# Two transformer layers on one core: where the gate of layer 0 is folded, when the weight additions are sent, and how the gate's rows are multiplied

## The chip, the core and the metric

The kernel runs on one core of a Trainium2 chip. The core has five engines that run their own queues in order and wait for each other through semaphores: TensorE (PE in the profile, its weight loads PEld), VectorE (DVE), ScalarE (ACT), GpSimd (POOL), and SyncE (SP), which here only issues transfers. The metric is device time of the whole program in microseconds (us). Before the change three runs took 984.28, 980.25 and 982.10 us, a median of 982.1.

## What is computed

The reference adds two layers to x (8 batches of 256 rows of 512, float32). Only layer 0 is touched. Its conditioning is an attention with rotary positions over a window of 256 keys in a paged cache, and its feed-forward part is a gated sum of eight weight matrices, which differ in 4096 places:

```python
q = rope(rms(x @ Wq.T)); k = rope(rms(x @ Wk.T)); v = x @ Wv.T
# k and v are written into the cache's blocks at pos = kv_len + t
p = softmax(where(allowed, q @ k_all.T * SCALE, -inf))
h = concat_heads(p @ v_all) @ Wo.T                       # output of the attention

logits = clip(h @ gate_w.T, -50, 50)                     # 8 experts
top_w, top_idx = top_k(logits, 2);  rw = softmax(top_w)
weighted = (softmax(expert_atom_weights) @ atoms) * sigmoid(importance)   # 8 x 4096
vals = einsum('tk,tks->ts', rw, weighted[top_idx])
out = h @ W.T + segment_sum((h[:, cols] * vals).T, rows).T   # rows, cols from mask_idx
x = x + out
```

Layer 1 (a linear layer with low-rank adapters, then a mixture of eight experts, two per row) follows and isn't touched.

## The kernel before

**Tiles.** There are 16 tiles of 128 rows (NT), two to a batch; the 512 columns are four chunks of 128 (KC). All products are float32, and the profile records such a product as two records of PE; a transpose through PE is one.

**Projection (from L1147).** For each tile, `keys_values` (L1153) multiplies x by the weights of keys and values, rotates the keys on VectorE and stores them to kv_new in HBM. Beside it the eight weight matrices are laid out in HBM: `spread_base` (L1186) copies the common matrix eight times side by side and stores it to delta_d (16 stores, issued by SP), and `sum_same` (L1276) and `find_places` (L1301) find the sums and the places of the 4096 entries, in 32 columns. `add_delta` (L1127) sends one column of 128 entries to delta_d, as an indirect transfer that adds, issued by POOL. Six of these (BESIDE) are sent in the projection's loop, at tiles 8 to 13. The weights woT (output projection) and gw (gate) are fetched at tile 8 by `later` (L1307).

At its end the projection makes the queries of batches 0 and 1: `query_rows` (L1092) multiplies and rotates, `queries_turned` (L1114) transposes on PE and copies out with ScalarE.

**Fold.** The gate sees only the attention's output, so its weights are multiplied with the output projection once: gwo = Wo.T @ gate_w.T, 512 x 8. Before the attention's loop (L1490 to L1509) the four blocks of woT are transposed (pw), copied out (won), and each serves as the stationary operand of four products with 8 columns (pgo):

```python
for k in range(KC):
    nc.tensor.matmul(pgo[k], won[:, k * P : (k + 1) * P], gw[:, d, :], start=(d == 0), stop=(d == KC - 1))
```

**Attention (loop over 8 batches, from L1526).** Batch b works on keys and values that were gathered by POOL into kv_rows[b] (`gather_old` from the cache, `gather_new` from kv_new, four indirect transfers each), two batches ahead. `prepared` transposes the next batch's keys (KT) and makes its masks, `queries` projects the batch after next, `attend` makes scores (ps), softmax on VectorE and ScalarE (s), transposes (pp, pT) and products with values (po), for one tile and eight heads at a time. Between a batch's two tiles five of the remaining additions (LATER) are issued by POOL; each of them waits until the one before has landed.

After a batch's two tiles, `gate_rows(i)` (L1476) makes the logits of one tile: four products with a 128 x 128 stationary piece of the attention's output oT and the 8 columns of gwo, summed in PSUM, then one VectorE operation clips them into lg0. `output_rows` (L630) multiplies the tile by woT and stores h. Then the queries of batch b + 2 are turned.

**What sets the order.** The source gives dependences; a planner with costs of its own orders each engine's instructions when the program is built, and each engine then runs its list strictly in that order. PSUM is cut into pools with a fixed number of buffers: in the projection psq (3), psd (3, and two single buffers pw0 and pw1), in the attention ps_s (2), ps_p (2) and ps_o (2, tag misc, shared by pg, ph, pk, pt, po). `in_a_row` (L107) keeps the products given to it next to each other, so that products on different halves or quarters of the array's columns can run side by side. `seen_through` (L116) is a helper that layer 1 uses for its own fold: it is printed below.

Of the kernel before, what the change touches and what calls it, by code (L numbers as in the profile page):

```python
# [19 lines left out]
P = 128  # L20
B, T, D = 8, 256, 512
# [3 lines left out]
KC = D // P  # L25
# [6 lines left out]
E = 8  # L32
# [3 lines left out]
NSC = NS // P  # L36
# [45 lines left out]
def two_layer_kernel(ctx: ExitStack, tc: tile.TileContext, io: dict, out: bass.AP):  # L82
    nc = tc.nc
# [514 lines left out]
    ost = ExitStack()  # L598
    op = ost.enter_context(tc.tile_pool(name="op", bufs=1, side="right"))
    woT = op.tile([P, KC, D], F32, name="woT")  # L600
    gwo = op.tile([P, KC, E], F32, name="gwo")
    oTs = {}

    def load_delta(half, pool, engines, bufs, tag="raw", paced=False):
# [41 lines left out]
    with ExitStack() as att:  # L646
        ap = att.enter_context(tc.tile_pool(name="ap", bufs=1))
# [7 lines left out]
        sums = place_ap.tile([P, NSC, E], F32, name="sums")  # L655
# [9 lines left out]
        minus_half = ap.tile([P, 1], F32, name="minus_half")  # L665
        nc.gpsimd.memset(minus_half, -0.5)

        gw = ap.tile([P, KC, E], F32, name="gw")
        epss = ap.tile([P, 2], F32, name="epss")
        nc.gpsimd.memset(epss[:, 0:1], EPS)  # L670
        nc.gpsimd.memset(epss[:, 1:2], EPS / (SCALE * SCALE))
# [442 lines left out]
        def queries_turned(qrs, psum, tag):  # L1114

            QT = qtp.tile([P, KC, T], F32, name="QT")
            for t, qr in enumerate(qrs):
                qflat = qr.rearrange("p h d -> p (h d)")
                pt = psum.tile([P, KC, P], F32, name="pt", tag=tag)
                for m in range(KC):  # L1120
                    nc.tensor.transpose(
                        pt[:, m, :], qflat[:, m * P : (m + 1) * P], ident
                    )
                nc.scalar.copy(QT[:, :, t * P : (t + 1) * P], pt)
            return QT

        def add_delta(k, values):  # L1127

            nc.gpsimd.indirect_dma_start(
                out=delta_d,  # L1130
                out_offset=bass.IndirectOffsetOnAxis(ap=put_i[:, k : k + 1], axis=0),
                in_=values,
                in_offset=None,
                bounds_check=D * D + P - 1,
                oob_is_err=True,
                compute_op=ALU.add,
            )
# [2 lines left out]

        roots = ap.tile([P, NT, H], F32, name="roots")

        BESIDE = 6
        LATER = 5


        with proj:  # L1147
# [159 lines left out]
            def later(tile, src, rs):  # L1307

                nc.scalar.copy(tile[:, 0, :1], rs[:, :1])
                nc.sync.dma_start(tile, src)  # L1310

            FIRST = 8
            summed = placed = 0
            for i in range(LEAD, NT):
                rs = keys_values(i)
                if i == LEAD:
                    with_gains(qcos, qsin, "q_scale")
                    rot.close()
# [12 lines left out]
                for k in range(summed, min(summed + 3, NSC)):  # L1331
                    sum_same(k)
                    summed = k + 1
                if summed - placed >= 8 or i == NT - 1:
                    find_places(range(placed, summed))
                    placed = summed
                if i >= FIRST and i - FIRST < BESIDE:
                    add_delta(i - FIRST, sums[:, i - FIRST, :])
            gather_new(0)

            qq = proj.enter_context(tc.tile_pool(name="qq", bufs=2, side="right"))
            QTs = {}
            for b in range(2):
                rows = [
                    query_rows(
                        i, blocks[NTB][:, :, i * P : (i + 1) * P], psq, "pkv", qq, early=True
                    )
                    for i in range(2 * b, 2 * b + 2)
                ]
                QTs[b] = queries_turned(rows, psd, "psd")  # L1350


        otp = ost.enter_context(tc.tile_pool(name="otp", bufs=1, side="right"))
# [119 lines left out]
                if m % 2:  # L1473
                    next(beside, None)

        def gate_rows(i):  # L1476
            pg = ps_o.tile([P, E], F32, name="pg", tag="misc")
            for k in range(KC):
                nc.tensor.matmul(
                    pg,  # L1480
                    oTs[i // 2][:, k, (i % 2) * P : (i % 2 + 1) * P],
                    gwo[:, k, :],
                    start=(k == 0),
                    stop=(k == KC - 1),
                )
            nc.vector.tensor_scalar(lg0[:, i, :], pg, 50.0, -50.0, ALU.min, ALU.max)

        AHEAD = 2

        with ExitStack() as fold:  # L1490
            fo = fold.enter_context(tc.tile_pool(name="fo", bufs=1))
            pgos = [ps_s.tile([P, 2, 512], F32, name="pgo", tag="ps") for j in range(KC // 2)]
            pgo = [pgos[k // 2][:, k % 2, :E] for k in range(KC)]
            for d in range(KC):
                pw = ps_o.tile([P, KC, P], F32, name="pw", tag="misc")
                for k in range(KC):
                    nc.tensor.transpose(pw[:, k, :], woT[:, k, d * P : (d + 1) * P], ident)
                won = fo.tile([P, D], F32, name="won")
                nc.scalar.copy(won, pw.rearrange("p c r -> p (c r)"))
                for k in range(KC):  # L1500
                    nc.tensor.matmul(
                        pgo[k],
                        won[:, k * P : (k + 1) * P],
                        gw[:, d, :],
                        start=(d == 0),
                        stop=(d == KC - 1),
                    )
            for k in range(KC):
                nc.scalar.copy(gwo[:, k, :], pgo[k])  # L1509

        gather_new(1)
        ready = prepared(0, kv_rows[0])
        zero = wop.tile([P, D], F32, name="zero")
# [12 lines left out]
        for b in range(B):  # L1526
            kvs = kv_rows[b]
            if b + AHEAD < B:
                if b + AHEAD > 2:
                    find_rows(b + AHEAD)  # L1530
                gather_old(b + AHEAD)
                gather_new(b + AHEAD)
            if b == B - 2:
                beside = load_delta(0, xq, (nc.scalar.copy,), 3, tag="xb", paced=True)
                next(beside)
            oTs[b] = otp.tile([P, KC, T], F32, name="oT", bufs=4)
            if b + 2 < B:
                qrs = queries(b + 2)
            if b < B - 2:
                start_sums(b)  # L1540
            if b == B - 3:
                start_sums(b + 1)
                start_sums(b + 2)
            if b == 1:
                for rest in (*sums_d, h_d, g_d):
                    nc.sync.dma_start(rest[N:, :], zero)
            attend(b, 0, kvs, QTs[b], *ready, beside)
            now = ready
            if b + 1 < B:
                ready = prepared(b + 1, kv_rows[b + 1])  # L1550
            ks = range(BESIDE + LATER * b, min(BESIDE + LATER * (b + 1), NSC))
            if ks:

                held = bp.tile([P, 1], F32, name="held")
                nc.vector.tensor_scalar(held, ready[1][:, 0, :1], 1.0, None, ALU.is_lt)
                entries = bp.tile([P, len(ks), E], F32, name="entries")
                nc.vector.tensor_scalar(
                    entries, sums[:, ks[0] : ks[-1] + 1, :], held, None, ALU.mult
                )
                for j, k in enumerate(ks):  # L1560
                    add_delta(k, entries[:, j, :])
# [560 lines left out]
```

## Time and profile before

One execution was profiled. It took 983.58 us, its span from the first to the last instruction is 981.7 us, and its mean clock granted to TensorE is 0.967 of full speed.

| Stretch of the span, us | Length | PE busy | DVE busy | ACT busy | POOL busy | clock |
|---|---|---|---|---|---|---|
| 0 to 80, start and projection | 80 | 69.68 | 57.50 | 45.49 | 32.85 | 0.96 |
| 80 to 88 | 8 | 6.19 | 4.00 | 5.21 | 0.00 | 0.57 |
| 88 to 111, projection's end | 23 | 20.90 | 20.85 | 14.20 | 8.80 | 1.00 |
| 111 to 129, fold and first query rows | 18 | 17.32 | 9.42 | 3.60 | 13.96 | 0.53 |
| 129 to 138 | 9 | 6.88 | 7.72 | 3.19 | 5.64 | 1.00 |
| 138 to 143 | 5 | 4.37 | 5.00 | 3.60 | 1.10 | 0.66 |
| 143 to 412, attention | 269 | 257.56 | 184.15 | 181.64 | 104.48 | 1.00 |
| 412 to 460, output rows and routing | 48 | 39.41 | 32.20 | 14.67 | 14.81 | 0.89 |

How to read the profile: a line of a list by time gives start and length in us, engine, line of the kernel, operation, output and inputs by the program's names with their shapes, and how many instructions are merged; in brackets stands the idle time of that engine before it and what released it. [...]the pace of a series is read from one start to the next. "DMA_INDIRECT" on POOL is a gather or a scatter[...].

### The profile page before, as it was taken

How to read it: one execution, taken by the hardware profiler on the slowest of the kernel's cores; microseconds unless marked ns; L12 is line 12 of the kernel's file. 1: busy time of each engine (PE TensorE's matmuls, PEld its weight loads, DVE VectorE, ACT ScalarE, POOL GpSimd, SP SyncE). 2: the span in 40 equal slices, each digit the busy share in tenths (PEclk: the TensorE clock that was granted, in tenths of full speed). 3: DMA queues.
4: the chain of work that ended last, by engine and by line, in shares of the span. 5: the costliest groups of instructions: out<-in, count | busy, mean ns of one | idle time of the engine just before them, and what ended most of it. 6: DMA issues, size and time to landing. Idle time of an engine off the chain costs nothing. (4 is left out here: it accounts for less than half of the span.)

```text
span 981.7 us, 14436 instructions
## 1 busy us (share of the span) xinstructions
PE 914.2 (93%) x4897; PEld 511.9 (52%) x4897; DVE 455.7 (46%) x1477; ACT 372.5 (38%) x958; POOL 357.2 (36%) x333
## 2 busy tenths in 40 slices
PE   6998889999999998897999997999599999999995
PEld 3554646556556565545433333545277777753332
DVE  5786789758548576583211111471012222323332
ACT  3675447547557489651111112410111111112321
POOL 2631655654554300123666652000223333333211
PEclk9898789999999999997999999999799999999998
DMA  6696494423441202256997766981433444343322
GB/s 192 216 320 236 123 306 143 115 59 82 118 126 28 93 19 70 84 195 226 344 308 139 126 111 144 357 315 43 171 74 67 70 73 73 65 75 62 49 28 37
DMA packets 74238, 134.63 MB, mean 137 GB/s; under 512 B 17309, under 2 KB 22941, under 8 KB 74032
## 3 DMA queue, kind: packets, MB, share of 16 engines
q0 software_dynamic: 25088, 43.68, 23.5%
q1 hardware_dynamic: 38496, 74.57, 21.9%
q10 hardware_dynamic: 10576, 15.39, 4.3%
q8 instruction: 42, 0.69, 0.3%
q14 instruction: 36, 0.29, 0.1%
HBM read 89.95 MB, written 52.56 MB: 145 GB/s over the span
## 5 line engine op out<-in xcount | busy, mean ns | idle before, releaser
L575 DVE COPY xsT<-pa 128x512 f32<-128x512 f32 x68 | 46.8, 688 | 155.6 <-PE pa L569 148.5
L533 POOL DMA_INDIRECT xs<-g_d,token_i_l x34 | 35.3, 1037 | 229.4 <-PE pa L569 129.4
L2014 DVE TENSOR_TENSOR y<-py,b 64x512 f32<-64x512 f32 (+1 forms) x46 | 31.7, 690 | 185.8 <-PE py L547 122.2
L1998 ACT ACTIVATE hs<-pu,b 128x64 f32<-128x64 f32 (+1 forms) x184 | 46.2, 348 | 185.8 <-PE pu L1972 144.4
L556 PE MATMUL py<-delta,xsT 128*64 128x512 f32 (+1 forms) x416 | 94.8, 598 | 0.0
L1439 ACT ACTIVATE s<-s,mx,roots 128x384 f32<-128x384 f32 x128 | 89.7, 705 | 12.2 <-DVE mx L1435 11.3
L1972 PE MATMUL pu<-xsT,w 128*128 128x128 f32 x704 | 82.9, 276 | 0.0
L1972 PEld LDWEIGHTS pu<-xsT,w 128*128 128x128 f32 x704 | 80.9, 193 | 0.4 <-issue 0.4
L547 PE MATMUL py<-w,hs 128*128 128x512 f32 x176 | 79.3, 593 | 0.0
L1158 PE MATMUL pkv<-wkv,xb 128*128 128x512 f32 x128 | 66.9, 648 | 8.5 <-DMA wkv<-wqkvT 8.5
L580 POOL DMA_INDIRECT out<-y,token_i_l x34 | 54.0, 1587 | 55.6 <-DVE y L2015 51.2
L1462 PE MATMUL po<-pT,kv 128*64 128x128 f32 x768 | 66.0, 283 | 7.1 <-ACT pT L1457 7.1
L1423 DVE CUSTOM_DVE_ANT_0 s<-ps,mask 128x384 f32<-128x384 f32 x128 | 67.1, 551 | 11.8 <-PE ps L1408 10.0
L1788 ACT ACTIVATE y<-py,weight_l 128x512 f32<-128x512 f32 x34 | 23.4, 688 | 126.1 <-PE py L556 86.9
L1462 PEld LDWEIGHTS po<-pT,kv 128*64 128x64 f32 x768 | 46.0, 136 | 43.1 <-ACT pT L1457 35.8
L580 POOL DMA_INDIRECT sums_d<-y,token_i_l x34 | 53.9, 1586 | 31.4 <-ACT y L1788 13.8
L1408 PE MATMUL ps<-KT,QT 64*128 64x384 f32 x256 | 59.1, 541 | 4.2 <-DVE mx L1423 4.0
L1457 ACT COPY pT<-pp 128x384 f32<-128x384 f32 x128 | 55.9, 478 | 16.7 <-PE pp L1453 15.8
L1453 PE MATMUL pp<-ident,s 128*128 128x128 f32 x384 | 59.9, 283 | 2.5 <-DVE s L1450 2.4
L569 PEld LDWEIGHTS pa<-ident,xs 128*128 128x128 f32 x272 | 32.7, 145 | 53.8 <-issue 48.4
L569 PE MATMUL pa<-ident,xs 128*128 128x128 f32 x272 | 43.6, 286 | 18.1 <-DMA xs<-g_d,token_i_l 11.4
L1096 PE MATMUL pq<-wq,xb 128*128 128x512 f32 x128 | 59.7, 614 | 0.0
(385 smaller groups left out, 1546.4 us busy)
## 6 DMA issues: line engine op xcount, KB each, us to landing
delta_d<-spread SPq DMA_DIRECT2D x16, 512.0 KB, 4.8
raw<-delta_d SPq DMA_DIRECT2D x16, 512.0 KB, 4.6
w<-fc_w SPq DMA_DIRECT2D x8, 1024.0 KB, 19.4
w<-fc_w SPq DMA_DIRECT2D x16, 512.0 KB, 17.3
part<-sums_d SPq DMA_DIRECT2D x32, 256.0 KB, 4.8
xb<-xT SPq DMA_DIRECT2D x5, 1024.0 KB, 6.4
sums_d<-zero SPq DMA_DIRECT2D x18, 256.0 KB, 5.4
kv_new<-kvt ACTq DMA_DIRECT2D x16, 256.0 KB, 2.7
```

What stands on the lines that cost most here:

```text
L547: nc.tensor.matmul(py, xT[:, k, :], of_expert(experts[0])(weights(k)), start=(k == 0), stop=(k == KC - 1),)
L556: lambda k=k, h=h: nc.tensor.matmul(py[h * HR : (h + 1) * HR, :], xT[:, k, h * HR : (h + 1) * HR], of_expert(experts[h])(weights(k)), star ...
L569: nc.tensor.transpose(dst[:, k, :], src[:, k * P : (k + 1) * P], ident)
L580: nc.gpsimd.indirect_dma_start(out=sum_d, out_offset=bass.IndirectOffsetOnAxis(ap=token_i[:, s : s + 1], axis=0), in_=y, in_offset=None, b ...
L1096: nc.tensor.matmul(pq, xcols[:, k, :], wq[:, k, :], start=(k == 0), stop=(k == KC - 1))
L1158: nc.tensor.matmul(pkv, xb[:, k, cols], wkv[:, k, :], start=(k == 0), stop=(k == KC - 1),)
L1408: lambda r=r: nc.tensor.matmul(pss[r], QT[r * HD : (r + 1) * HD, m, t * P : (t + 1) * P], KT[r * HD : (r + 1) * HD, u, t * P : t * P + WU] ...
L1423: nc.vector.tensor_tensor_reduce(out=s, in0=pss[r], in1=mask[:, t, :], scale=1.0, scalar=NEG, op0=ALU.add, op1=ALU.max, accum_out=mx[:, r ...
L1439: nc.scalar.activation(ss[r], ss[r], AF.Exp, bias=mx[:, r : r + 1], scale=root[:, r : r + 1], accum_out=sm[:, r : r + 1],)
L1453: nc.tensor.transpose(pp[:, c * P : (c + 1) * P], s[:, c * P : (c + 1) * P], ident)
L1462: lambda c=c, r=r: nc.tensor.matmul(po[r * HD : (r + 1) * HD, :], kvs[t + c][:, v0 + r * HD : v0 + (r + 1) * HD], pTs[r][:, c * P : (c + 1 ...
L1972: nc.tensor.matmul(pu[:, c, :], w1[:, k, plan.full[s], c * P : (c + 1) * P], xsT[:, k, :], start=(k == 0), stop=(k == KC - 1),)
```

## The change

1. The fold moves from the attention into the end of the projection, after the query rows of batch 1 are made and before they are turned, and it takes the form that layer 1 uses (`seen_through`): the transposed block wn is the moving operand of one product of 512 columns, the gate's weights are the stationary one, 32 columns wide (8 and zeros), and the four products land in four quarters of one PSUM bank. One copy, four transposes and one sum over the quarters on VectorE make gwo. gw and gwo become 32 columns wide and are cleared by POOL.
2. The six additions of the projection's loop go; LATER is 6 instead of 5.
3. `gate_rows` works on a batch. gwo is the stationary operand, 32 columns in each of the four quarters of the array, and the batch's 256 rows move through; the parts are copied out by VectorE, transposed on PE, summed over the quarters and clipped.

```diff
-    gwo = op.tile([P, KC, E], F32, name="gwo")
+    gwo = op.tile([P, KC, BW], F32, name="gwo")
+    nc.gpsimd.memset(gwo, 0.0)
...
-        gw = ap.tile([P, KC, E], F32, name="gw")
+        gw = ap.tile([P, KC, BW], F32, name="gw")
+        nc.gpsimd.memset(gw, 0.0)
...
-        BESIDE = 6
-        LATER = 5
+        LATER = 6
...
-                nc.sync.dma_start(tile, src)
-
-            FIRST = 8
+                nc.sync.dma_start(tile[:, :, : src.shape[-1]], src)
...
-                if i >= FIRST and i - FIRST < BESIDE:
-                    add_delta(i - FIRST, sums[:, i - FIRST, :])
             gather_new(0)
...
-                QTs[b] = queries_turned(rows, psd, "psd")
+                if b == 0:
+                    QTs[b] = queries_turned(rows[b], psd, "psd")
+
+            seen_through(
+                gwo[:, :, :E],
+                lambda o: [woT[:, k, o * P : (o + 1) * P] for k in range(KC)],
+                gw,
+                qq,
+                lambda name, shape: psd.tile(
+                    shape, F32, name=name, tag="pw0" if name == "acc" else "psd",
+                    bufs=1 if name == "acc" else 3,
+                ),
+                nc.scalar.copy,
+            )
+            QTs[1] = queries_turned(rows[1], psd, "psd")
...
-        def gate_rows(i):
-            pg = ps_o.tile([P, E], F32, name="pg", tag="misc")
-            for k in range(KC):
-                nc.tensor.matmul(
-                    pg,
-                    oTs[i // 2][:, k, (i % 2) * P : (i % 2 + 1) * P],
+        def gate_rows(b):
+            pg = ps_o.tile([P, T], F32, name="pg", tag="misc")
+            in_a_row(
+                lambda k=k: nc.tensor.matmul(
+                    pg[k * BW : (k + 1) * BW, :],
                     gwo[:, k, :],
-                    start=(k == 0),
-                    stop=(k == KC - 1),
-                )
-            nc.vector.tensor_scalar(lg0[:, i, :], pg, 50.0, -50.0, ALU.min, ALU.max)
+                    oTs[b][:, k, :],
+                    start=True,
+                    stop=True,
+                )
+                for k in (3, 2, 1, 0)
+            )
+            parts = sp.tile([P, T], F32, name="parts", bufs=1)
+            nc.vector.tensor_copy(parts, pg)
+            pt = ps_o.tile([P, T // P, P], F32, name="pt", tag="misc")
+            for t in range(T // P):
+                nc.tensor.transpose(pt[:, t, :], parts[:, t * P : (t + 1) * P], ident)
+            lg = lg0[:, 2 * b : 2 * b + 2, :]
+            nc.vector.tensor_reduce(
+                lg,
+                pt.rearrange("p t (o c) -> p t c o", o=KC)[:, :, :E, :],
+                AX.X,
+                ALU.add,
+            )
+            nc.vector.tensor_scalar(lg, lg, 50.0, -50.0, ALU.min, ALU.max)
...
-        with ExitStack() as fold:
-            ...
-            for d in range(KC):
-                pw = ps_o.tile([P, KC, P], F32, name="pw", tag="misc")
-                for k in range(KC):
-                    nc.tensor.transpose(pw[:, k, :], woT[:, k, d * P : (d + 1) * P], ident)
-                won = fo.tile([P, D], F32, name="won")
-                nc.scalar.copy(won, pw.rearrange("p c r -> p (c r)"))
-                ...
-            for k in range(KC):
-                nc.scalar.copy(gwo[:, k, :], pgo[k])
...
-            ks = range(BESIDE + LATER * b, min(BESIDE + LATER * (b + 1), NSC))
+            ks = range(min(LATER * b, NSC), min(LATER * (b + 1), NSC))
...
             attend(b, 1, kvs, QTs[b], *now, beside)
+            gate_rows(b)
             for i in range(2 * b, 2 * b + 2):
-                gate_rows(i)
                 if i < EARLY:
                     output_rows(i, ps_o, sp)
```

More of the change, by code (lines that the diff above doesn't have):

```diff
@@ L1336, in two_layer_kernel @@
                     placed = summed
-                if i >= FIRST and i - FIRST < BESIDE:
-                    add_delta(i - FIRST, sums[:, i - FIRST, :])
             gather_new(0)
             qq = proj.enter_context(tc.tile_pool(name="qq", bufs=2, side="right"))
-            QTs = {}
+            QTs, rows = {}, {}
             for b in range(2):
-                rows = [
+                rows[b] = [
                     query_rows(
@@ L1482, in gate_rows @@
                     gwo[:, k, :],
-                    start=(k == 0),
-                    stop=(k == KC - 1),
-                )
-            nc.vector.tensor_scalar(lg0[:, i, :], pg, 50.0, -50.0, ALU.min, ALU.max)
-        AHEAD = 2
-        with ExitStack() as fold:
-            fo = fold.enter_context(tc.tile_pool(name="fo", bufs=1))
-            pgos = [ps_s.tile([P, 2, 512], F32, name="pgo", tag="ps") for j in range(KC // 2)]
-            pgo = [pgos[k // 2][:, k % 2, :E] for k in range(KC)]
-            for d in range(KC):
-                pw = ps_o.tile([P, KC, P], F32, name="pw", tag="misc")
-                for k in range(KC):
-                    nc.tensor.transpose(pw[:, k, :], woT[:, k, d * P : (d + 1) * P], ident)
-                won = fo.tile([P, D], F32, name="won")
-                nc.scalar.copy(won, pw.rearrange("p c r -> p (c r)"))
-                for k in range(KC):
[L1501 to L1506, printed above, removed]
-                    )
-            for k in range(KC):
-                nc.scalar.copy(gwo[:, k, :], pgo[k])
```

## The prediction

> **What bounds the kernel now.** I read in this order: the page's busy shares, the row of granted clock, the busy times by stretch, then the list by time of each engine around the edits. The page's chain that ended last covers under 1% of the span (it breaks off at the last scatter), so it carries nothing here.
>
> ```profile
> PE 914.2 (93%) x4897; PEld 511.9 (52%) x4897; DVE 455.7 (46%) x1477; ACT 372.5 (38%) x958; POOL 357.2 (36%) x333
> ...
> PEclk9898789999999999997999999999799999999998
> ```
>
> TensorE is the engine to shorten, but its clock dips in a few slices, one of them the fifth (98 to 123 us), where the gate's fold stands. By stretch (the numbers after the length: busy time of PE, PEld, DVE, ACT, POOL, then clock):
>
> ```profile
> core 0: us, PE busy (x) PEld busy (x) DVE busy (x) ACT busy (x) POOL busy (x), PEclk, DMA share, GB/s
> 220.00:257.00 37.00, 36.91 (x237) 21.93 (x236) 22.85 (x79) 21.55 (x58) 19.25 (x16) 1.00 0.34 87
> 372.00:412.00 40.00, 33.20 (x278) 22.39 (x278) 22.66 (x93) 36.63 (x77) 1.45 (x8) 1.00 0.20 55
> ```
>
> In the middle batches of the attention PE has 0.1 us of idle in 37: whatever leaves PE there shortens the kernel. In the last batch ACT (36.6 of 40) sets the pace. Around the fold:
>
> ```profile
> 112.00:124.00 12.00, 11.85 (x54) 11.03 (x55) 4.53 (x12) 3.11 (x10) 9.49 (x10) 0.50 0.56 144
> 124.00:128.00 4.00, 4.00 (x8) 1.93 (x8) 3.33 (x11) 0.00 (x0) 3.09 (x4) 0.50 0.94 304
> ```
>
> For 16 us PE is busy and at half clock. PE's list by time (start, length, then in brackets the idle time before):
>
> ```profile
> 108.15 0.60 PE L1121 MATMUL pt<-ident,qr 128*128 128x128 f32 x4
> 110.84 0.63 PE L1121 MATMUL pt<-ident,qr 128*128 128x128 f32 x4 [2.10 <-DVE qr L1090]
> 112.15 1.97 PE L1497 MATMUL pw<-ident,woT 128*128 128x128 f32 x8 [0.68 <-ACT QT L1124]
> ...
> 115.72 1.09 PE L1497 MATMUL pw<-ident,woT 128*128 128x128 f32 x4
> ...
> 124.43 9.05 PE L1096 MATMUL pq<-wq,xb 128*128 128x512 f32 x16
> 133.42 1.56 PE L1408 MATMUL ps<-KT,QT 64*128 64x384 f32 x8
> ```
>
> PE waits 2.1 us for VectorE's rotated queries of batch 1, the clock halves, the whole fold and part of the next query projection run at half speed, and the attention starts at 133.42.
>
> **Part 1, the fold moves ahead of batch 1's turned queries.** In the new program's order PE goes from the last projection of tile 3 (it ends near 108.15) straight into the fold, then turns batch 1's queries, then keys, then the next projection. Costs at full clock: four transposes take 0.43 us (104.28 to 104.71), a 512-column product of two records 0.86 (eight records in 3.44, 104.71 to 108.15).
> Before, 108.15 to 133.42 is 25.3 us: at full clock 13.8 (8+16+8 transposes 3.4; 32 records of 8 columns at 0.108, 3.5; 16 projection records 6.9), idle 2.8, half clock about 7.9 (half of 15.85 busy us), small gaps the rest.
> After: 16 transposes 1.7, four 512-column products 3.4, four transposes 0.4, then 8 query and 8 key transposes 1.7, projection 6.9: 14.2. New waits: each product waits for a ScalarE copy (0.59), two of these copies stand behind one square that waits for VectorE; the four last transposes wait for the copy of the sum. I step through these by the rows above and get 1.5 us. 15.7, so PE reaches the attention 9.6 us earlier. The projection's rows of x are there: issued at 108.46 when tile 3 is done, landed 5.3 later, at 113.8, wanted at about 117.
> What is late next is VectorE. It stood idle in the old order, for the keys that came behind the fold:
>
> ```profile
> 122.07 0.69 DVE L1381 COPY KT<-pk 128x512 f32<-128x512 f32 x1 [6.51 <-PE pk L1378]
> ...
> 134.79 0.55 DVE L1423 CUSTOM_DVE_ANT_0 s<-ps,mask 128x384 f32<-128x384 f32 x1
> ```
>
> Its idle time from 115.6 to 134.8 sums to 9.9 us (6.5, 1.6, 1.5, 0.2). The new reduce into gwo (0.29, the same operation in layer 1) stands in VectorE's order before a mask, and would wait some 1.6 us for the transposes, with masks and key copies queued behind it. So at most 9.9 - 1.6 - 0.3 = **8.0 us** are got back, less than PE's 9.6; I take 8.0.
> [...] The trace shows 16 us at half clock under work that the profile calls busy[...]. [...]the clock came back about 4 us into the 512-column projection[...] 16 transposes now stand in a row before the projection, with a wait ahead of them. If the clock falls there, half of 4 us, 2 us, goes. The measured row decides the 7.9; the 2 us stays in the range.
>
> **Part 2, the additions.** Six scatter-additions leave the projection; each later batch has six instead of five, batch 5 two instead of one.
>
> ```profile
> 105.88 1.65 POOL L1129 DMA_INDIRECT delta_d<-sums,put_i  x1 [2.27 <-ACT QT L1124]
> 107.83 1.09 POOL L1058 DMA_INDIRECT kv<-kv_new,idx_new  x1 [0.30 <-issue]
> ...
> 114.63 1.00 POOL L1058 DMA_INDIRECT kv<-kv_new,idx_new  x1 [0.31 <-issue]
> ```
>
> They come every 3.9 us, each waiting for the one before to land, and batch 0's gathers stood between them: the last was issued at 114.63 and lands 3.6 later, at 118. The keys' transposes would now be wanted at about 116, so without this edit 2 us of part 1 would go. With it four gathers at 1.3 us follow the last kv_new store (101.7 plus 2.7) and land by 113. In the attention the sixth costs POOL 1.6 us and up to 2.3 of waiting per batch; POOL is busy 104 us of the 269 from 143 to 412, and what queues behind (roots, gathers of the batch after next) is wanted a batch later. The last addition lands about 4 us later within its batch; the first read of the sums follows it on SP, but the first copy of such a read starts 47 us after that read was issued (316.2 to 363.2). Nothing. If the cover were gone: 3.9 us per batch.
>
> **Part 3, gate rows by batch.** Two old tiles:
>
> ```profile
> 163.13 1.06 PE L1479 MATMUL pg<-gwo,oT 128*128 128x8 f32 x8
> 164.04 0.53 PE L1453 MATMUL pp<-ident,s 128*128 128x128 f32 x3
> ...
> 616.60 1.08 PE L1846 MATMUL px<-x1T,aTg 128*32 128x128 f32 x32 [0.68 <-ACT x1T L1840]
> 617.61 0.66 PE L1839 MATMUL pt<-ident,part 128*128 128x128 f32 x4
> ```
>
> One tile takes 0.91 us (start to start), the second 0.81: 1.72 a batch. The nearest row to the new form is layer 1's inner product on quarters: 32 records of 128 columns in 1.01 us, where one after the other they would take 32 x 0.107 = 3.4. So eight groups of four side by side, 0.86, plus 0.15. [...] New: two groups of 256 columns, 0.43, plus 0.15, plus two transposes 0.21: 0.79. **Gain 0.93 a batch.** If the quarters ran in turn: 8 x 0.215 + 0.21 = 1.93, a loss of 0.2.
> New waits: the transposes wait for VectorE's copy of 128x256 (estimate 0.42, the time of L1087's 128x256 products), behind them stand both output rows, the turned queries and the next projection. Five transposes and two scores (0.55 + 0.85) lie between in most batches, more than the copy; the second output row waits for the reduce, behind 1.7 us of the first. I cost it at nothing; bare, it is 0.4 to 1.5 us a batch.
> Sum: batches 1 to 5, bound by PE, 5 x 0.93 = 4.65; batch 0, where VectorE is busy 33 of 37 us, 0.6; batch 6 0.5; batch 7 -0.5 (ACT-bound, and the routing waits for its last logits through one more copy and reduce). **5.2 us.** Two POOL memsets (0.2 each) fall into its idle time from 5 to 21.9 us: nothing.
>
> **Sum.** 8.0 + 5.2 = 13.2. The profiled execution took 983.6 (span 981.7): 970.4. The median is 1.5 below it: **969 us**. The stages behind start on the attention's end and should move whole.
>
> **Rivals.**
> A, both parts work (0.60): 964 to 974.
> B, only the fold pays (0.16): quarters in turn or waits eat part 3: 982 - 8 = 974, to 976.
> C, only the rows pay (0.07): VectorE, already 100% busy from 130 to 150, turns the earlier start into waiting and the clock dips again there: 982 - 5 = 977. For it: PE idles 2.1 us at 137 and the clock is down at 138 to 142 already now.
> D, nothing measurable (0.09): ACT, which copies the fold's pieces in order, or the transfers of the projection (PE stands 3.5 us at 78 us behind a ScalarE copy that waits for a store; the order of these copies shifts by one or two) give it back: 979 to 985.
> E, slower (0.08): the two-way chain PE-VectorE-PE-VectorE in each batch. If the copy stands behind a softmax pass (0.74 + 0.63) without the cover, 2.2 us a batch with the latencies; PE stands, and a gap of that size is what halved the clock at 110. It decides from 13.2/8 = 1.7 us a batch on; at 2.2 the time is 982 - 13 + 18 = 987, with 2 us lost to half clock in three of the batches 993. Against it: the cover above, VectorE's 14 us of slack a batch.
>
> **How the numbers follow.** 0.5% (4.9 us) is about what a measurement can tell from no change. Faster: A, B and most of C, 0.82; within: D and edges, 0.11; slower 0.07. The range reaches from A's low end with some room (962: if the clock also stays up at the start of the attention) over B and C to 979. A's own is 964 to 974.
>
> **What would show it.** Right: no half clock between 108 and 126, first scores near 125, the first softmax pass on VectorE near 127; pg groups of 8 records in 0.5 to 0.6 us and no idle before L1506; attention's last gate near 399. Wrong: idle on PE before the transposes of parts or before ph; half clock in the new fold; POOL late with gathers so that key transposes wait.

## The result: 975.0 us against 982.3, and the profile after

The changed kernel took 975.0 us (median of 12 runs, 970.1 to 979.0) against 982.3 (12 runs beside it). The ratio is 0.9918, with a 95% interval of 0.9898 to 0.9937. The forecast was 969 with a range of 962 to 979. The time lies in the range and the direction is right, but of the 13.2 us forecast only 7.3 came (6.2 to 10.0 by the interval). The profiled execution was the fastest of the twelve, 970.1 us (span 968.4), so its trace flatters the kernel. The trace of before has half clock from 80.7 to 87.5 us, which of the other traces only that of run 2 below has too (82.7 to 86.1). So it is chance that the two traces lie 13.3 us apart, as much as was forecast. A second trace of the changed kernel (run 11) is used below.

The busy shares and the granted clock on the page of the changed kernel:

```profile
PE 901.9 (93%) x4829; PEld 491.8 (51%) x4829; DVE 455.5 (47%) x1487; ACT 371.8 (38%) x954; POOL 360.3 (37%) x335
...
PEclk9899999999999999997999999999799999999998
```

TensorE is busy for 12.3 us less than before. The stretches that answer to those shown before (busy time of PE, PEld, DVE, ACT, POOL, then clock):

```profile
112.00:124.00 12.00, 10.22 (x41) 5.19 (x39) 11.24 (x33) 1.67 (x3) 8.85 (x9) 1.00 1.01 334
124.00:128.00 4.00, 1.33 (x9) 0.31 (x5) 4.00 (x16) 2.86 (x5) 2.78 (x2) 1.00 0.97 329
208.00:245.00 37.00, 36.41 (x229) 20.43 (x228) 24.09 (x89) 21.55 (x57) 21.95 (x17) 1.00 0.40 98
360.00:400.00 40.00, 30.83 (x250) 18.91 (x249) 21.86 (x94) 34.20 (x68) 2.52 (x19) 0.96 0.17 47
```

The half clock of 111 to 129 us is gone, and VectorE is now the full engine there (11.24 of 12, then 4.00 of 4). A middle batch is still bound by TensorE (36.41 of 37). In the last 40 us of the attention the clock is 0.96 (half clock from 388.3 to 391.7); before, it was 1.00 there, and half clock of the same length began at 411.8, just behind the last output. TensorE's list around the fold:

```profile
105.27 1.26 PE L123 MATMUL pw<-ident,woT 128*128 128x128 f32 x10
106.55 1.53 PE L126 MATMUL acc<-wn,gw 128*32 128x512 f32 x4
108.01 0.88 PE L123 MATMUL pw<-ident,woT 128*128 128x128 f32 x6
109.17 1.53 PE L126 MATMUL acc<-wn,gw 128*32 128x512 f32 x4 [0.29 <-ACT wn L125]
111.38 0.66 PE L133 MATMUL pt<-ident,parts 128*128 128x128 f32 x4 [0.68 <-ACT parts L130]
...
115.79 7.13 PE L1098 MATMUL pq<-wq,xb 128*128 128x512 f32 x16 [1.05 <-DVE KT L1393]
122.85 1.56 PE L1420 MATMUL ps<-KT,QT 64*128 64x384 f32 x8
```

From the end of tile 3's projection to the first scores it is 17.6 us (105.27 to 122.85), before 25.3 (108.15 to 133.42). The gate's rows of a middle batch:

```profile
191.34 0.64 PE L1493 MATMUL pg<-oT,gwo 128*32 128x256 f32 x8
191.91 0.77 PE L1465 MATMUL pp<-ident,s 128*128 128x128 f32 x5
...
193.45 0.44 PE L1506 MATMUL pt<-ident,parts 128*128 128x128 f32 x2
193.72 7.03 PE L635 MATMUL ph<-woT,oT 128*128 128x512 f32 x16
```

Start to start they take 0.57 + 0.27 = 0.84 us, before 1.72, and TensorE doesn't wait for the copy between them.

### The profile page after: what moved, and what is told of

Its sections match the earlier page's. It is cut to its first block, busy times and chain, and to the rows that moved or that the text cites. A ratio compares the mean times of both kernels' runs of the same rounds, so it can differ in the third digit from the quotient of the medians.

```text
span 968.4 us, 14307 instructions
## 1 busy us (share of the span) xinstructions
PE 901.9 (93%) x4829; PEld 491.8 (51%) x4829; DVE 455.5 (47%) x1487; ACT 371.8 (38%) x954; POOL 360.3 (37%) x335
## 5 line engine op out<-in xcount | busy, mean ns | idle before, releaser
L533 POOL DMA_INDIRECT xs<-g_d,token_i_l x34 | 35.2, 1035 | 230.1 <-PE pa L569 129.5
L1474 PE MATMUL po<-pT,kv 128*64 128x128 f32 x768 | 69.4, 285 | 6.4 <-ACT pT L1469 6.4
L1131 POOL DMA_INDIRECT delta_d<-entries,put_i x32 | 53.1, 1660 | 53.3 <-DMA delta_d<-entries,put_i 38.6
L580 POOL DMA_INDIRECT sums_d<-y,token_i_l x34 | 54.2, 1593 | 31.6 <-ACT y L1794 17.2
```

Source lines behind the costliest of these rows:

```text
L580: nc.gpsimd.indirect_dma_start(out=sum_d, out_offset=bass.IndirectOffsetOnAxis(ap=token_i[:, s : s + 1], axis=0), in_=y, in_offset=None, b ...
L1474: lambda c=c, r=r: nc.tensor.matmul(po[r * HD : (r + 1) * HD, :], kvs[t + c][:, v0 + r * HD : v0 + (r + 1) * HD], pTs[r][:, c * P : (c + 1 ...
```

## The experiments

Each run was timed beside the kernel before on its chip.

| kernel | median us | before beside it | ratio (95% interval) |
|---|---|---|---|
| changed | 975.0 | 982.3 | 0.9918 (0.9898 to 0.9937) |
| 1: fold and additions, rows by tiles | 973.9 | 980.7 | 0.9924 (0.9897 to 0.9951) |
| 2: rows alone | 981.3 | 980.7 | 1.0007 (0.9985 to 1.0030) |
| 3: before, hole filled | 987.5 | 980.7 | 1.0051 (1.0024 to 1.0079) |
| 4: fold and rows, additions put back | 980.4 | 980.7 | 1.0001 (0.9971 to 1.0032) |
| 5: new place, old form of the fold | 976.3 | 981.3 | 0.9917 (0.9885 to 0.9950) |
| 6: old place, new form | 975.1 | 981.3 | 0.9931 (0.9896 to 0.9965) |
| 7: additions alone | 982.2 | 981.3 | 1.0006 (0.9984 to 1.0028) |
| 8: last batch's rows by tiles | 974.5 | 981.3 | 0.9903 (0.9872 to 0.9934) |
| 9: rows by batch twice | 983.6 | 982.9 | 1.0004 (0.9982 to 1.0026) |
| 10: rows by tiles twice | 994.2 | 982.9 | 1.0129 (1.0096 to 1.0161) |
| 11: changed, again | 971.6 | 982.9 | 0.9897 (0.9863 to 0.9931) |
| 12: last two batches' rows by tiles | 969.8 | 982.2 | 0.9866 (0.9825 to 0.9907) |

### 1 and 2: which part pays

Run 1 is the changed kernel with the old `gate_rows(i)` for each tile; run 2 is the kernel before with the new `gate_rows(b)`:

```diff
 # run 1, from the changed kernel
-            gate_rows(b)
             for i in range(2 * b, 2 * b + 2):
+                gate_rows(i)      # the old form, on gwo[:, k, :E]
 # run 2, from the kernel before
+            gate_rows(b)          # the new form
             for i in range(2 * b, 2 * b + 2):
-                gate_rows(i)
-                won = fo.tile([P, D], F32, name="won")
+                won = sp.tile([P, D], F32, name="won", tag="h", bufs=2)
```

> The changed kernel with the gate's rows by tiles, as before (parts 1 and 2 without part 3). The changed kernel measured 975.0 against 982.3. Theory F (the fold's place makes nearly the whole gain, the rows by batch lose in new waits what they save on TensorE): 974 to 976. Theory H (fold and rows each give about half, 3.5 us): 978 to 979. My forecast as it stood (fold 8.0, rows 5.2): 974, and then the sum of the parts would not fit the measured 975.

> The kernel before with the gate's rows by batch on quarters alone (part 3 alone; the fold stays at the attention's start with products of 8 columns, its copied blocks in two buffers in place of one). Theory F: 981 to 983, no difference. Theory H: 978 to 979. My forecast as it stood: 977.

Run 1 gave 0.9924, some 7.5 us, as much as all three parts together; run 2 gave nothing. Theory F holds in its numbers and H falls. The forecast for the fold (8.0) fits run 1; the 5.2 us for the rows appear in neither comparison. F's reason, that new waits eat the rows' saving in each batch, is looked at in 8 to 12.

### 7 and 4: the additions

```diff
 # run 7, from the kernel before
-        BESIDE = 6
-        LATER = 5
+        BESIDE = 0
+        LATER = 6
 # run 4, from the changed kernel: the reverse, six in the projection's loop
+                if i >= FIRST and i - FIRST < BESIDE:
+                    add_delta(i - FIRST, sums[:, i - FIRST, :])
```

> The kernel before with the additions alone moved: none beside the projection, six a batch (part 2 alone). With the additions left in, the other two parts together gave nothing (980.4 against 980.7), so part 2 decides over some 5 us beside the new fold. Theory G (it only lets batch 0's gathers land 5 us sooner, and in the old order the keys are wanted after they land): no difference, 0.998 to 1.001. Rival (fewer transfers and additions beside the projection pay by themselves): 0.994 to 0.996, the gain of part 2 is then not tied to the fold.

> The changed kernel with the additions put back: six beside the projection, five a batch after it (parts 1 and 3 without part 2). My forecast: batch 0's gathers from the new keys land near 118 in place of 113, the keys' transposes wait for them, 2 us slower than the changed kernel: 977. Rival (the wait is hidden behind VectorE, which is the limit there): 975, no difference.

Alone the additions' move gives nothing (1.0006, theory G). Beside the new fold it decides: with the six additions put back, the changed kernel is as slow as the one before. Run 4 misses both expectations, by 5 and 7 us when each is taken relative to the kernel before. Its list by time, of TensorE and then of POOL:

```profile
113.26 0.33 PE L1394 MATMUL pk<-ident,kv 128*128 128x128 f32 x1 [0.73 <-ACT QT L1126]
116.11 0.33 PE L1394 MATMUL pk<-ident,kv 128*128 128x128 f32 x1 [2.52 <-DMA kv<-kv_new,idx_new]
118.02 0.47 PE L1394 MATMUL pk<-ident,kv 128*128 128x128 f32 x1 [1.58 <-DMA kv<-kv_new,idx_new]
119.74 1.33 PE L1394 MATMUL pk<-ident,kv 128*128 128x128 f32 x5 [1.25 <-DMA kv<-kv_new,idx_new]
121.07 8.58 PE L1098 MATMUL pq<-wq,xb 128*128 128x512 f32 x16
129.58 1.56 PE L1424 MATMUL ps<-KT,QT 64*128 64x384 f32 x8
```

```profile
106.76 1.09 POOL L1060 DMA_INDIRECT kv<-kv_new,idx_new  x1 [0.30 <-issue]
111.34 1.58 POOL L1131 DMA_INDIRECT delta_d<-sums,put_i  x1 [3.48 <-ACT parts L130]
113.23 1.24 POOL L1060 DMA_INDIRECT kv<-kv_new,idx_new  x1 [0.31 <-issue]
114.78 1.04 POOL L1060 DMA_INDIRECT kv<-kv_new,idx_new  x1 [0.30 <-DMA delta_d<-sums,put_i]
116.12 1.00 POOL L1060 DMA_INDIRECT kv<-kv_new,idx_new  x1 [0.30 <-issue]
```

An addition stands between batch 0's first gather and the other three, and waits 3.48 us from 107.9 on; the profile names ScalarE's copy of the fold's parts (L130) as what ended the wait; why it should wait for that copy isn't shown. TensorE then waits 2.5, 1.6 and 1.3 us for the keys, 5.4 in all, and its clock is half again from 117.2 to 124.0 us. Of these 6.8 us 2.9 fall into the projection, which takes 8.58 us in place of 7.13. First scores stand at 129.6, 7 us behind the changed kernel.

### 3, 5 and 6: the hole, the place and the form of the fold

```diff
 # run 3, from the kernel before, ahead of batch 1's queries_turned
+                if b == 1:
+                    idle = psd.tile([P, 512], F32, name="idle", tag="psd")
+                    for n in range(6):
+                        nc.tensor.matmul(idle, blocks[NTB][:, n % KC, 3 * P : 4 * P],
+                                         wq[:, n % KC, :], start=True, stop=True)
 # run 5, from the changed kernel, in place of seen_through(...)
+            for d in range(KC):   # the old loop: 4 transposes, a copy, 4 products of 8 columns
 # run 6, from the changed kernel: seen_through(...) taken out of the projection's end
         AHEAD = 2
+        seen_through(gwo[:, :, :E], ..., gw, sp, ..., nc.scalar.copy, tag="h", bufs=2)
```

> The kernel before with six products of 512 columns more (2.6 us at full clock, their result is not used), which stand in TensorE's order in the hole of 2.1 us ahead of batch 1's turned queries, the rest as before. Theory K (the hole lets the clock fall, and the half clock is what the fold's old place cost): no half clock from 111 to 128, first scores 7 to 8 us earlier, 975 to 977 in all. Rival W (the fold's place and form cost by their own work and waits, the clock follows the kind of work, transposes and products of 8 columns, and falls all the same): half clock still there, 982 to 983.

> The changed kernel with the fold at its new place but in the old form: sixteen products of 8 columns onto four sums, no parts, no last transposes. The kernel before was 980.7 beside the four runs so far, the changed kernel stands at 0.992 of it (973 to 975). Theory P (the place decides: no hole on TensorE ahead of the fold, so the clock stays up in either form): 0.991 to 0.994 of before, no half clock between 105 and 120. Rival Q (the form decides: transposes and products of 8 columns let the clock fall wherever they stand): half clock in or behind the fold, 0.998 to 1.002.

> The changed kernel with the fold in the new form (quarters of the columns, 512 columns a product) but at the old place, at the attention's start; its blocks share the buffers of the output rows. Theory P: the hole of 2.1 us ahead of batch 1's turned queries is back, the clock falls, 0.998 to 1.002 of before. Rival Q: the products of 512 columns keep the clock up, or bring it back after one window of 3.4 us: 0.992 to 0.995.

What the clock did, by stretches of each trace (columns as above). Run 7, where the fold is that of the kernel before:

```profile
104.00:108.00 4.00, 3.32 (x16) 2.65 (x14) 3.75 (x10) 1.37 (x3) 3.29 (x3) 0.50 0.69 234
108.00:112.00 4.00, 4.00 (x20) 3.81 (x20) 0.63 (x3) 0.98 (x2) 3.23 (x5) 0.50 1.05 361
112.00:116.00 4.00, 4.00 (x21) 3.63 (x19) 0.85 (x2) 0.87 (x4) 2.16 (x3) 0.50 1.02 380
116.00:121.00 5.00, 5.00 (x13) 2.93 (x13) 3.29 (x11) 0.38 (x4) 3.61 (x5) 0.50 0.99 340
```

Run 6, the new form at the old place, with TensorE's line behind the hole:

```profile
106.66 0.63 PE L1123 MATMUL pt<-ident,qr 128*128 128x128 f32 x4 [2.16 <-DVE qr L1092]
104.00:108.00 4.00, 1.16 (x10) 0.72 (x8) 4.00 (x10) 2.16 (x5) 3.08 (x4) 0.97 0.75 219
108.00:112.00 4.00, 4.00 (x13) 2.06 (x14) 3.96 (x14) 1.28 (x3) 3.39 (x3) 0.61 1.06 354
112.00:116.00 4.00, 3.03 (x17) 1.53 (x17) 1.46 (x5) 1.66 (x3) 3.23 (x5) 1.00 0.81 236
```

Run 5, the old form at the new place, with TensorE's line behind the fold:

```profile
115.60 1.97 PE L1401 MATMUL pk<-ident,kv 128*128 128x128 f32 x8 [3.39 <-issue]
105.00:109.00 4.00, 3.98 (x34) 3.45 (x33) 3.53 (x8) 2.08 (x5) 3.20 (x3) 1.00 0.64 183
109.00:113.00 4.00, 2.98 (x26) 2.65 (x24) 1.62 (x3) 1.33 (x3) 3.28 (x4) 1.00 1.10 376
113.00:117.00 4.00, 1.40 (x7) 1.41 (x8) 0.81 (x3) 1.48 (x7) 3.23 (x4) 0.63 0.90 267
```

In run 6 the hole is back (2.16 us ahead of batch 1's last turned rows) and the clock falls at 107.7, but with products of 512 columns behind it it is full again at 111.2 (half clock of 3.4 us stands in the trace of before as well, from 138.7 to 142.1). In run 7, with the same hole and products of 8 columns, it stays at half for 17 us in which TensorE is busy nearly throughout. In run 5 there is no hole and the products of 8 columns run at full clock from 105 to 113; the clock falls only at 114.0, inside a wait of 3.39 us behind the fold (its releaser is not shown in the trace). In all the traces with half clock at the fold (before and runs 2 to 7) it ends 1.3 to 4.1 us after the next products of 512 columns begin, and never ahead of them. So neither P nor Q alone fits: behind the hole the clock fell, and under the old form it stayed down.

By the times, taking away either is enough (0.9917 and 0.9931). The traces bear that out in part only. From the end of tile 3's projection to the first softmax pass the kernel before takes 26.6 us, run 5 22.4, run 6 21.9 and the changed kernel 19.3. And these are single executions: run 5's trace is of its slowest (981.9 us), run 7's of one of its fastest (975.9), and in run 6 the later batches are ordered anew as well (batch 3 takes 42.0 us, in the changed kernel 37.8).

Run 3 bears it out for the fold and not beyond. The filling took 5.15 us, twice what I had reckoned, because each product is two records. The fold then ran at full clock from 111 to 117 us, with waits of 0.2 to 0.7 us for its copies. From 117.5 to 124.3 the clock was half, and it fell just before a wait of 1.07 us for a gather began: under the old form the small waits may be enough, which is not shown. From the end of tile 3's projection to the first scores it took 25.5 us, before 25.3, and not 7 to 8 less: 5.1 us of clock came back, but the filling took 3.05 us more than the hole, and the fold now waited for its copies. Behind that the planner had laid out the attention anew, with a batch 3 of 42.4 us in place of 38.9. Its 987.5 us therefore say little about the hole, and both expectations for the total miss.

### 11, 9 and 10: what the rows cost

Run 11 is the changed kernel unaltered. Runs 9 and 10 make the rows twice, the first time into a tile that is not read:

```diff
 # run 9, from the changed kernel; again: a tile of its own in place of lg0
+            gate_rows(b, again)
             gate_rows(b)
 # run 10, from run 1
+                gate_rows(i, again)
                 gate_rows(i)
```

> The changed kernel itself, on the chip of the two others, for a second trace. The measured median was 975.0 where the profiled execution took 970.1. If the difference lies in windows of half clock that come and go (Theory K): this trace has two or three windows of 1.7 us more or fewer of them, and the batches of the attention as in the first trace to 0.5 us each. Rival: the attention's batches differ from the first trace by more than that.

> The changed kernel with each batch's gate rows made twice by batch on quarters, the first time into a tile that nobody reads. TensorE's own price in the changed kernel's trace is 0.57 + 0.27 = 0.84 us a batch. Theory M (TensorE sets the pace where rows are made, the price is TensorE's): 4 to 7 us slower than the changed kernel beside it, half of what the tiles cost twice. Rival N (the chain from TensorE to VectorE and back twice costs more than TensorE's time, so both forms cost the same): 10 to 14 us slower.

> The changed kernel with the gate's rows by tiles, as before, and each tile's rows made twice, the first time into a tile that nobody reads. TensorE's own price is 0.91 + 0.81 = 1.72 us a batch. The same kernel with rows once measured 0.992 of before. Theory M: 10 to 14 us slower than that, 1.002 to 1.006 of before. If the rows by tiles fill time in which TensorE waits anyway: 3 to 7 us slower, 0.995 to 0.999, and the saving forecast for part 3 was never there.

From each trace I take the start of every sixteenth softmax pass on VectorE (a batch has 16), then the last attention output (oT), then the routing's first maximum (L488). A batch's rows are made behind the next batch's first passes, so intervals 1 to 6 hold the rows of batches 0 to 5.

| trace | batch 0 | intervals 1 to 6 | sum 1 to 6 | batch 7 to last oT | to the maximum |
|---|---|---|---|---|---|
| before (tiles) | 22.0 | 39.4 38.7 38.9 38.8 37.3 26.8 | 219.9 | 34.2 | 7.0 |
| run 7 (tiles) | 21.8 | 39.1 38.7 38.9 38.7 37.3 26.9 | 219.6 | 34.2 | 7.0 |
| run 1 (tiles) | 26.3 | 37.2 39.0 38.9 38.7 37.3 26.8 | 217.9 | 35.3 | 7.2 |
| changed | 24.1 | 36.6 38.8 37.8 38.7 35.5 25.6 | 213.0 | 36.0 | 5.4 |
| changed again | 26.2 | 36.4 38.8 37.6 38.8 35.5 25.6 | 212.7 | 37.1 | 7.3 |
| run 2 (rows) | 22.5 | 39.1 37.7 38.8 37.3 35.2 25.6 | 213.7 | 36.1 | 9.2 |

The two traces of the changed kernel agree to 0.2 us in each of the intervals 1 to 6; they differ in batch 0 (by 2.1) and batch 7 (by 1.1), where windows of half clock come and go (25.5 us lost over the span in the second trace, 20.4 in the first, three windows of 1.7). Run 11's theory K holds for intervals 1 to 6.

The rows by batch do save: against run 1, which has the same fold, 4.9 us over six batches, 0.8 a batch (5.2 by the second trace; run 2 against before 6.2). Run 10 says the same from the other side: with the tiles' rows made once more, its intervals 1 to 6 sum to 228.7 us, 10.8 above run 1. That is 1.8 a batch, about TensorE's own price of 1.72, and not time in which it waits anyway. The whole costs 18.8 us against run 1 (994.2 against 0.9924 x 982.9 = 975.4), above the 10 to 14 of theory M; of the rest, 6.3 lies in batch 7 and the stretch to the maximum (48.8 against 42.5). Run 9 costs 12.0 against run 11, more than M's 4 to 7 and within rival N's 10 to 14. It is no clean price: its intervals 1 to 6 sum to 223.0, 1.7 more a batch, but in three of these batches TensorE waits ahead of the second set's transposes (1.27, 1.28 and 0.67 us), and in its trace the last logits come 7.4 us behind the last output in place of 2.8.

So the saving is there up to interval 6, and F's reason, new waits in each batch, falls. What is lost is lost between there and the routing's start, or behind it.

### 8 and 12: where the saving goes

```diff
 # run 8; run 12 has B - 2 and b >= B - 2
-            gate_rows(b)
+            if b < B - 1:
+                gate_rows(b)
             for i in range(2 * b, 2 * b + 2):
+                if b == B - 1:
+                    tile_rows(i)   # the old form
```

> The changed kernel with the last batch's gate rows by tiles as before, batches 0 to 6 by batch. In the profile of the changed kernel the last logits stand 2.75 us behind the last attention output, by tiles 1.0 to 1.8, and nothing else runs then. Theory: 1 to 2 us faster than the changed kernel, 0.990 to 0.991 of before. Rival (the routing's other work sets its start): no difference, 0.992.

> The changed kernel with the gate's rows of batches 6 and 7 by tiles, as before; batches 0 to 5 by batch. TensorE's order in batch 7 is then that of the kernel before: the last scores stand spread out, not eight records together. In the traces so far batch 7 with the stretch to the routing's first maximum takes 41.2 to 42.5 us by tiles and 41.4 to 46.1 by batch, with half clock inside batch 7 in all of the latter. Theory R (rows by batch save their 0.8 us in batches 1 to 6, and batch 7's new order with its half clock gives half of it back): batch 7 and that stretch 41 to 42.5, no half clock inside batch 7 before its last output, batch 6 back at 26.8, and 0.987 to 0.990 of before. Rival S (the saving is lost behind the attention, whatever batch 7 does): 0.991 to 0.993, as the changed kernel, or with the rows by tiles throughout.

In run 8 the last logits stand 1.0 us behind the last output, as wanted, but batch 7 takes 38.1 us, with half clock from 386.3 to 393.1: 45.1 us to the maximum, no better than the changed kernel. Its 0.9903 is what its theory had named, but its interval holds the changed kernel's 0.9918 too, and its trace doesn't show that reason. The tail is not it. TensorE's list in batch 7 of the changed kernel:

```profile
381.47 1.56 PE L1420 MATMUL ps<-KT,QT 64*128 64x384 f32 x8
384.65 0.85 PE L1465 MATMUL pp<-ident,s 128*128 128x128 f32 x6 [1.62 <-DVE s L1462]
387.24 0.43 PE L1474 MATMUL po<-pT,kv 128*64 128x128 f32 x2 [1.73 <-ACT pT L1469]
387.60 0.44 PE L1465 MATMUL pp<-ident,s 128*128 128x128 f32 x2
387.96 1.29 PE L1474 MATMUL po<-pT,kv 128*64 128x128 f32 x10
389.19 1.12 PE L1465 MATMUL pp<-ident,s 128*128 128x128 f32 x4
...
398.00 0.64 PE L1493 MATMUL pg<-oT,gwo 128*32 128x256 f32 x8 [0.38 <-DVE oT L1484]
399.47 0.44 PE L1506 MATMUL pt<-ident,parts 128*128 128x128 f32 x2 [0.83 <-DVE parts L1503]
```

With batch 6's rows by batch the planner puts two of the last scores together (8 records at 381.47), and TensorE then waits 1.6 and 1.7 us with little between; the clock falls at 388.3, and the transposes and products behind run slow (1.12 for four transposes, where full clock takes 0.66). All seven traces with batch 6's rows by batch, made once, have this order, these two waits, and 3.4 or 6.8 us of half clock inside batch 7. None of the five with both last batches by tiles (before, runs 1, 3, 7 and 12) has the order or the waits; their half clock there, 3.4 to 10.2 us of it, begins between 2.5 us ahead of the last output and 1.0 us behind it. Run 12's batch 7 has the old order:

```profile
382.04 0.92 PE L1420 MATMUL ps<-KT,QT 64*128 64x384 f32 x4
384.16 1.25 PE L1474 MATMUL po<-pT,kv 128*64 128x128 f32 x12 [1.21 <-ACT pT L1469]
385.34 0.87 PE L1465 MATMUL pp<-ident,s 128*128 128x128 f32 x6
...
388.04 0.66 PE L1465 MATMUL pp<-ident,s 128*128 128x128 f32 x4
...
393.31 1.06 PE L1519 MATMUL pg<-gwo,oT 128*128 128x8 f32 x8
```

Its longest wait there is 1.38 us, the clock is full until the last output, batch 7 takes 34.5 us and the stretch behind it 7.0. Intervals 1 to 6 sum to 213.3 (interval 6 stays at 25.6 and not at 26.8, since it holds batch 5's rows). The whole took 969.8 us, 0.9866 of before. Theory R holds (but for interval 6), S falls, and run 12 is the fastest of all. Against the changed kernel it is 3 to 5 us faster by the medians' ratios (0.9866 against 0.9897 and 0.9918), at the edge of what the intervals can tell (3.0 give or take 5.2, and 5.1 give or take 4.4). The loss isn't in every execution: the changed kernel's first trace takes 213.0 and then 41.4 us to the maximum, as run 12 does (213.3 and 41.4); its second takes 44.3 for the latter.

## Why the forecast was right and wrong

**What bounds the kernel.** Right: what left TensorE in the middle batches shortened them, 4.9 us over six.

**Part 1, the fold: 8.0 forecast.** Right. From the end of tile 3's projection to the first softmax pass it was 26.6 us before (108.15 to 134.79) and is 19.3 (105.27 to 124.55): 7.4 less, and 7.5 in the times of run 1 (give or take 2.7). That it fits so closely is in part luck: some of it is given back in batch 0, which grows from 22.0 us to 26.3 in run 1 (24.1 and 26.2 in the changed kernel), while interval 1 shrinks by 2.2. Over both, run 1 is 2.1 us slower than before. In its trace the clock is half there from 127.0 to 133.8 us; before it was half from 138.7 to 142.1. Such a dip behind an earlier start is what rival C had described (though VectorE was busy for 19.05 us of the 20 from 130 to 150, and not all the time).

That VectorE would be late next is seen in its 11.24 of 12 us. TensorE's own step was 17.6 us and not 15.7: the waits came to 2.8 us (0.29, 0.68, 0.73, 1.05) where I had 1.5. The 2 us that I kept in the range for a fall of the clock behind the transposes in a row were an estimate; it did not fall there (1.00 from 104 to 128).

To price the half clock by the measured row (7.9 us) was right: the gain forecast with it was 8.0, and 7.4 came. What holds the clock down for so long is not shown. Run 7 has 17 us of half clock under work, transposes and products of 8 columns; in run 5 the same mix ran at full clock from 105 to 113, and in run 6 the clock that fell at 107.7 was full again at 111.2.

**Part 2, the additions: "2 us of part 1 would go" without it.** The mechanism was right and the size was off. Run 4 against the changed kernel shows 8 us (1.0001 against 0.9918, give or take 3.6). I had priced the lateness of the last gather, and neither the addition's own wait of 3.5 us in POOL's order, nor the clock, which was half again from 117.2 to 124.0 us, behind TensorE's waits.

**Part 3, gate rows by batch: 5.2 forecast.** The price was right: 0.84 us a batch where I had 0.79, quarters side by side (0.57 us for the eight records, where I had 0.43 + 0.15), no waits in the middle batches. (VectorE's copy took 0.42 us as estimated, but the line with 128x256 products is L1081 and not L1087.) For batches 0 to 5 I had 0.6 + 4.65 = 5.25, and intervals 1 to 6 show 4.9. The step that failed is "batch 6 0.5; batch 7 -0.5". Batch 7 with the stretch to the routing's maximum takes 41.4 to 46.2 us in the seven traces with batch 6's rows by batch (run 8 among them; mean 44.3) and 41.2 to 42.5 in the five with both last batches by tiles (mean 41.7). That is 2.6 us given back, where the two terms together had nothing. I had counted the longer tail (the last logits 2.75 us behind the last output, before 1.0), and not that the planner would order the batch anew and that half clock would then fall inside it. Run 12, which puts these two batches back to tiles, takes 0.9866 of before, 13.2 us less (9.1 to 17.2 by its interval). That this is the sum forecast for the whole change is chance. The traces leave the rows 4.9 - 2.6 = 2.3 us on balance. By the times it is 0.6 us (changed against run 1, give or take 3.3, both intervals taken together), 2.7 (run 11 against run 1, give or take 4.3) and -0.7 (run 2, give or take 2.2): the first two have room for 2.3, the third just not. Whether a last microsecond goes behind the routing's start stays open: from the maximum to the end the seven traces take 561.9 to 567.9 us (mean 564.9), the five 563.6 to 566.8 (mean 564.3). The parts together, 7.4 for the fold less up to 2.1 in batches 0 and 1, and 2.3 for the rows, make 7.6 to 9.7 us, inside the 6.2 to 10.0 of the measurement.

**Rivals.** The time lies in B's window, only the fold pays (974 to 976), but not for its reason: quarters ran side by side and the waits were hidden. Of E's mechanism the gap behind a softmax pass that is followed by half clock was seen, but once, in batch 7, where TensorE waits for the softmax and not for the rows' copy, and for 2.6 us in all and not 2.2 in each batch.

## What to carry to other kernels

Price a change not only by the instructions that go, but by the holes that its new order leaves on TensorE: in the kernel before, a wait of 2.1 us was followed by 17 us at half clock (111.4 to 128.4), 8.5 us of work, where transposes and products of 8 columns came next. A saving that is right in the middle of a loop can be lost in its last turn, where another engine sets the pace (here ScalarE, busy 34.20 of 40 us); look at the first and the last batch by themselves. An edit that is worth nothing alone (the additions) can be the condition for another's whole gain.

## What the runs showed of the hardware

Summed over stretches of 1 us, the dips of the clock cost, in order, 3.4, 3.4, 8.5, 1.7, 1.7, 5.1 and 5.1 us of full clock in the trace of before, 3.4, 1.7, 5.1, 1.7 and 5.1 in the changed kernel's first, and 3.4, 1.7, 3.4, 5.1, 1.7 and 5.1 in run 12's, each time without the last one. Over the runs, the span times (1 - granted clock) averages 32.1 us for the kernel before (44 runs) and 25.0 for the changed kernel (12 runs): a difference of 7.1, as much as that of the times, and within one kernel its standard deviation (3.7 and 3.5) is as large as that of the times (3.2 and 2.8). The two go together: their correlation over the runs is 0.83 in both kernels.

In these traces the length of a wait doesn't settle whether the clock falls. Just behind the first scores TensorE waits 2.1 to 3.0 us in all fourteen traces. In thirteen of them half clock begins inside this wait or within 1.8 us of its end; in the changed kernel's first trace, after 2.42 us, it doesn't, and its batch 0 takes 24.1 us where the second trace has 26.2. Nor did it fall behind waits of 2.14 us (changed kernel, ahead of 81.68) and 2.69 (run 3, ahead of 80.81) in the projection.

An edit that only adds work can move the planner's order far behind it: in run 3 batch 3 took 42.4 us in place of 38.9.
